# A two-layer graph network on one core: sums of the router weights by one product, and the order of the queues around both routings

## The chip, the core and the metric

The kernel runs on one core of a Trainium2 chip. A core has a matrix engine (PE in the profile, with its weight loads as PEld), a vector engine (DVE), a scalar engine (ACT), a general engine (POOL, GpSimd) and a queue engine (SP) that issues transfers; DVE, ACT, POOL and SP each run their instructions in the order in which they are queued. Sixteen DMA engines move data between the chip's main memory and the core's. The metric is the device time of one execution in microseconds, the median of several runs; less is better.

## The reference

384 nodes with 1024 features pass through two layers, all in float32. Each layer adds two branches to x and then a mixture of experts. Cut to what matters here:

```
xn = layernorm(x)
x = x + graph_attention(xn, edges) + linear_attention(xn)          # layer 0
xn = layernorm(x)
q, k, v = split(xn @ wqkv.T)                                        # 8 columns each
logits = sum(softmax(q[e] * k[j]) * v[j])                           # per expert e
two best experts by logits, weights = softmax of the two logits
x = x + sum(weights * (silu(a) * g) @ w2[e].T),  a, g = xn @ w1[e].T
xn = layernorm(x)                                                   # layer 1
x = x + graph_convolution(xn, W, a, edges) + attention_with_norm(xn)
f = layernorm(x)
e = argmax(f @ centroids.T), alpha = sigmoid of that product
x = x + f + alpha * (relu(xhat * gamma[e] + beta[e]) @ w1[e] ...) @ w2[e] + b2[e] ...
```

Each router works on a normalized row. (x - mean) * rinv @ w is rinv * (x @ w) - mean * rinv * (sum of w over the features), so the kernel multiplies the raw rows with the router's weights and needs the feature sums of the weights once: `wsum` for `wqkv` (24 columns), `csum` for the centroids (8 columns).

## The kernel before

The nodes are three blocks of 128 rows (`nb`), the features eight chunks of 128 (`kc`). Weights stream in 2 MB loads on SP (`load_w`, `load_t`) through a ring of buffers: three to begin with, a fourth (`w_top`), two more (`w_more`) after layer 0's attention, and three more (`w_last`) before layer 1's second routing. A load is issued when the buffer that it takes has been read for the last time. The program is traced in the order of the code; a planner then orders each engine's queue by its own estimates of when operands are ready, so an instruction may stand ahead of others that were traced before it. `tc.issue_after(i)` puts the instructions of its block, on i's engine only, behind i. `held(loads, until)` makes loads wait until another instruction, here a gather, has landed. A pool of tiles opened where another was closed waits for that whole pool by default; with `reuse_waits="tile"` each tile waits only for the tiles that lay where it lies.

The stages that matter, by their times in the profiled execution:

- Start (0 to 17 us). Three blocks of x are loaded and normalized (`norm_on_both`: DVE one half, L204, ACT the other, L205), transposed on PE (`to_t`, L218, copies L219: DVE the first four chunks, ACT the rest) and then multiplied by the first weight (L135). Ahead of the transposes PE multiplies `wr` with a matrix of ones, eight products of 24 columns (L442), and DVE copies the sum to `wsum` (L450).
- First routing (500 to 568 us). For each block, `to_router` (transposes, product with `wr`, norm), `to_places` (`route_block`: the logits from L356 on, an Exp on ACT in L363, both one-hot rows, `both` in L769; `place_both`: the rank of each node from products with triangular and full ones, L387, and the slots, L389 to L400; then POOL scatters the rows to `xg0`) and `to_first` (expert 0's rows gathered by a product, L775). For the last block nothing else is left for PE: it multiplies the centroids with ones, eight products (L789), whose copy to `csum` is L798 on DVE, ranks the nodes, and counts each expert's nodes in `too_many` with a product per block (L344; a maximum on DVE, L346). Then DVE and ACT copy expert 0's rows to `xe0` (L792, L793).
- Experts of layer 0 (`experts0_sorted`, 568 to 699 us). Expert by expert: rows (`rows_of`, POOL loads `xs`, L905), hidden values (L919), then output rows (L972), which go to memory. POOL gathers them back by slot (`take`, L309, summed on DVE in L999); `ways_back` (L937 to L952) prepares tables for the last two experts, which come back by a product (L1041).
- Head of layer 1 (699 to 760 us). Per block: the rows taken back (`take_back`), the norm, transposes (L218), and products with the two halves of `w_gnn` (L1058). The halves were loaded at 673.65 and 678.81.
- Second routing (935 to 976 us). `to_router`, `to_places` and `to_first` of their own (L1197, L1219 to L1230, L1234); `add_normed` on ACT (L193), the gate as a Sigmoid on ACT (L1254), scattered with the node numbers to `ig` by POOL, and `too_many` again.
- Experts of layer 1 (976 us to the end). Pairs of experts; 4 MB of first weights and 4 MB of second weights for each pair. Each product with the first weights (L1371) and the second (L1402) frees buffers for the next loads; the output rows are added to `out` by scatters.

Of the kernel before, what the change touches and what calls it, by code (L numbers as in the profile page):

```python
# [45 lines left out]
def gps_two_layers(ctx: ExitStack, tc: tile.TileContext, d, out: bass.AP):  # L46
# [153 lines left out]
    def norm_on_both(dst, src, mean, rinv):  # L200

        off = small.tile([P, 1], F32, tag="off", name="off")
        ve.tensor_scalar(off, mean, rinv, -1.0, op0=OP.mult, op1=OP.mult)
        first = ve.tensor_scalar(dst[:, :HB], src[:, :HB], mean, rinv, op0=OP.subtract, op1=OP.mult)  # L204
        ac.activation(dst[:, HB:D], src[:, HB:D], AF.Identity, bias=off, scale=rinv)  # L205
        return off, first

# [133 lines left out]
    def too_many(pool, tag, oh, cap):  # L341
        ps = pool.tile([P, HB], F32, tag=tag, name="total")
        for b in range(NB):
            mm(ps[:, :X], lhsT=ones_q, rhs=oh[:, b, :], start=b == 0, stop=b == NB - 1)  # L344
        most = small.tile([P, 1], F32, tag="pl_m", name="pl_m")
        ve.tensor_reduce(most, ps[:, :X], AX.X, OP.max)  # L346
        over = small.tile([P, 1], I32, tag="pl_o", name="pl_o")
        ve.tensor_scalar(over, most, float(cap), None, op0=OP.is_gt)
        return over

    def route_block(ps, sums, off, rinv, apart):
# [6 lines left out]
        qk = small.tile([P, X, X], F32, tag="r_qk", name="r_qk", bufs=1)  # L358
# [3 lines left out]
        ve.tensor_tensor(qk, qk, top[:, :, None].to_broadcast([P, X, X]), OP.subtract)  # L362
        ac.activation(qk, qk, AF.Exp)  # L363
        ready(AF.Sqrt, qk[:, 0, 0:1])
        tot = small.tile([P, X], F32, tag="r_s", name="r_s")
        ve.tensor_reduce(tot, qk, AX.X, OP.add)
        ve.reciprocal(tot, tot)
        ve.tensor_tensor(qk, qk, qkv[:, 2, None, :].to_broadcast([P, X, X]), OP.mult)
        logit = small.tile([P, X], F32, tag="r_l", name="r_l")
        ve.tensor_reduce(logit, qk, AX.X, OP.add)  # L370
# [45 lines left out]
    with ExitStack() as layer:  # L416
# [6 lines left out]
        with tc.tile_pool(name="edges", bufs=1) as ed, tc.tile_pool(name="hot", bufs=2) as hot, \  # L423
# [16 lines left out]
            ps = pa.tile([P, HB], F32, tag="mm", name="sums")  # L440
            for kc in range(KC):
                mm(ps[:, :3 * X], lhsT=ones_q, rhs=wr[:, kc, :], start=kc == 0, stop=kc == KC - 1)  # L442
            ready(AF.Sqrt, eps)
# [5 lines left out]
            with tc.issue_after(copied[0].ins):  # L449
                ve.tensor_copy(wsum, ps[:, :3 * X])  # L450

# [291 lines left out]
        with tc.tile_pool(name="ps_m0", bufs=4, space=PSUM) as pm, \  # L743
# [11 lines left out]
            def to_router(nb):  # L755
                gp.dma_start(x1[nb * P:(nb + 1) * P, :], x[:, nb, :])
                to_t(pm, xT, x[:, nb, :], nb)
                ps = px.tile([P, HB], F32, tag="x", name="x")
                for kc in range(KC):
                    mm(ps[:, :3 * X], lhsT=xT[:, kc, nb * P:(nb + 1) * P], rhs=wr[:, kc, :],  # L760
                       start=kc == 0, stop=kc == KC - 1)
                mean, rinv = norm_block(x[:, nb, :])
                off, _ = norm_on_both(xn[:, nb, :], x[:, nb, :], mean, rinv)
                ready(AF.Exp, xn[:, nb, D - 1:D])
                queries[nb] = (ps, wsum, off, rinv)

            def to_places(nb):
                oh = route_block(*queries[nb], share[:, 1, nb:nb + 1])
                ve.tensor_tensor(both[:, nb, :], oh[0], oh[1], OP.add)  # L769
                place_both(px, slots[:, nb, :], own0[:, nb, :], both, oh, nb)  # L770
                scatter(xg0[:, :], [slots[:, nb, i:i + 1] for i in range(2)], [xn[:, nb, :]] * 2, X * CAP0)

            def to_first(nb):
                for kc in range(KC):
                    mm(first[kc // 4][:, kc % 4, :], lhsT=xn[:, nb, kc * P:(kc + 1) * P], rhs=own0[:, nb, :],  # L775
                       start=nb == 0 and kc % 4 == 0, stop=nb == NB - 1 and kc % 4 == 3)

# [9 lines left out]
            ps = px.tile([P, HB], F32, tag="x", name="sums")  # L787
            for kc in range(KC):
                mm(ps[:, :X], lhsT=ones_q, rhs=cen[:, kc, :], start=kc == 0, stop=kc == KC - 1)  # L789
            to_places(NB - 1)  # L790
            to_first(NB - 1)
            ve.tensor_copy(keep["xe0"][0], first[0])  # L792
            ac.copy(keep["xe0"][1], first[1])  # L793
# [3 lines left out]
            ve.tensor_tensor(share[:, 1, :], share[:, 1, :], share[:, 0, :], OP.mult)  # L797
            ve.tensor_copy(csum, ps[:, :X])  # L798
            over0 = too_many(px, "x", both, CAP0)


# [89 lines left out]
    def experts0_sorted(keep):  # L891

        slots, share = keep["slots"], keep["share"]
        with tc.tile_pool(name="act6", bufs=1) as act, \
                tc.tile_pool(name="work6", bufs=2) as work, \
                tc.tile_pool(name="ps_h6", bufs=5, space=PSUM) as ph, \
                tc.tile_pool(name="ps_t6", bufs=3, space=PSUM) as pt:

# [67 lines left out]
            for hf in range(2):  # L966
# [15 lines left out]
                if hf == 0:  # L982
                    for nb in range(NB):
                        yt = work.tile([P, 2, HB], F32, tag="yt", name="yt6", bufs=3)
                        take(hf, nb, yt, slots, share, X * CAP0)
            take_back(work.tile([P, D], F32, tag="xs", name="yt1").rearrange("p (a b) -> p a b", b=HB), 0)

# [33 lines left out]
    def layer1(keep=None):  # L1021


        with tc.tile_pool(name="act2", bufs=1) as act, \
# [18 lines left out]
            for nb in range(NB):  # L1043
                with ExitStack() as behind:
                    if nb:
                        behind.enter_context(tc.issue_after(normed_half.ins))
                    if keep is not None:
                        if nb:
                            taken = take_back(work.tile([P, 2, HB], F32, tag="xn", name="yt1"), nb)
                        xs = x[:, nb, HB:]  # L1050
                        ve.tensor_tensor(xs, xs, backs[nb], OP.add)
                    mean, rinv = norm_block(x[:, nb, :])
                    _, normed_half = norm_on_both(xn1[:, nb, :], x[:, nb, :], mean, rinv)
                to_t(pm, xnT, xn1[:, nb, :], nb)
                for hf in range(2):
                    ps = pm.tile([P, HB], F32, tag="mm", name="mm")
                    for kc in range(KC):
                        mm(ps, lhsT=xnT[:, kc, nb * P:(nb + 1) * P], rhs=ws[hf][:, kc, :],  # L1058
                           start=kc == 0, stop=kc == KC - 1)
                    ac.copy(hn[:, nb, hf * HB:(hf + 1) * HB], ps)  # L1060
# [126 lines left out]
            own = keep["own"]  # L1187
            sums, last = {}, []

            def to_router(nb):  # L1190
# [350 lines left out]
```

## Time and profile before

| what | value |
|---|---|
| median of 3 runs | 1060.62 us (1059.91 to 1061.09) |
| profiled execution: time | 1058.17 us |
| profiled execution: span on the core | 1056.4 us |
| PE busy | 1019.2 us (96%) |
| DVE, ACT, POOL busy | 356.2, 270.6, 320.3 us |
| mean granted PE clock | 0.986 |
| moved by DMA | 182.83 MB, mean 173 GB/s |
| PE waits, first routing (550 to 590 us) | 2.5, 0.7, 0.5 and 0.4 us |
| PE waits, head of layer 1 (698 to 745 us) | 3.0, 1.9 (three times) and 0.7 us |
| PE waits, second routing and after (940 to 1057 us) | 2.4, 1.9 (twice), 1.4, 1.1 (twice), 0.4 and 0.3 us |

Lines such as L387 are lines of the kernel before. A row of the timeline gives the start, the length, the engine, the line and the operation, what is written and read, and in brackets the idle time before it and what ended that. Equal neighbours are drawn together (x16 is 16 records); one float32 product leaves two records on PE. A row of the table by stretches gives the busy times of PE, PEld, DVE, ACT and POOL with their counts, then the granted PE clock, the mean share of the DMA engines in use, and GB/s. A wait view gives the total, the count and the longest.

### The profile page before, as it was taken

The numbers are of one execution on the slowest core, as the hardware profiler recorded it, in microseconds if no ns is written. First come the engines' busy times: TensorE is split into PE (matmuls) and PEld (weight loads), VectorE is DVE, ScalarE is ACT, GpSimd is POOL, SyncE is SP. The second block draws the span as 40 slices with busy tenths as digits, with TensorE's granted clock in tenths as the row PEclk, the third lists the DMA queues.
The fourth block names the chain that finished last, engine by engine and source line by source line (L and its number), as shares of the span: only waits on it lengthen the run. The fifth ranks groups of instructions, "written<-read, shape, count | busy, mean of one in ns | idle before, by whom it ended". The sixth has DMA issues, their size and how long they took to land. (4 is left out here: it accounts for less than half of the span.)

```text
span 1056.4 us, 9529 instructions
## 1 busy us (share of the span) xinstructions
PE 1019.2 (96%) x3455; PEld 554.2 (52%) x3455; DVE 356.2 (34%) x993; ACT 270.6 (26%) x501; POOL 320.3 (30%) x277
## 2 busy tenths in 40 slices
PE   6999999999999999999998999989999999999995
PEld 5555555554455555544456666434444465656341
DVE  4580000007666766721333111043304100365321
ACT  3111111100776666621112101221212110113210
POOL 2142456566686678510001000050001100001231
PEclk9999999999999999999998999999999999998998
DMA  9939522424424342523155887969622222625994
GB/s 352 398 134 367 156 80 89 151 96 109 80 0 91 71 80 0 160 80 130 61 199 215 306 309 281 373 219 370 228 80 79 80 80 79 241 92 206 309 373 117
DMA packets 69525, 182.83 MB, mean 173 GB/s; under 512 B 21488, under 2 KB 22352, under 8 KB 69216
## 3 DMA queue, kind: packets, MB, share of 16 engines
q1 hardware_dynamic: 41072, 147.58, 38.6%
q0 software_dynamic: 25408, 29.93, 12.3%
q10 hardware_dynamic: 2992, 4.65, 1.2%
q8 instruction: 29, 0.48, 0.2%
q14 instruction: 24, 0.20, 0.1%
HBM read 160.22 MB, written 22.44 MB: 173 GB/s over the span
## 5 line engine op out<-in xcount | busy, mean ns | idle before, releaser
L482 POOL DMA_INDIRECT countd<-seen,cells x96 | 153.4, 1598 | 62.9 <-DMA countd<-seen,cells 37.7
L135 PE MATMUL mm<-xnT,w 128*128 128x384 f32 x512 | 165.7, 486 | 0.1
L135 PEld LDWEIGHTS mm<-xnT,w 128*128 128x128 f32 x512 | 97.1, 190 | 67.7 <-DVE xnT L219 0.4
L668 PE MATMUL mm<-xnT,w 128*128 128x384 f32 x384 | 132.4, 493 | 0.0
L482 POOL DMA_INDIRECT lastd<-typ,cells x96 | 96.7, 1007 | 108.4 <-DMA lastd<-typ,cells 70.9
L668 PEld LDWEIGHTS mm<-xnT,w 128*128 128x128 f32 x384 | 70.5, 190 | 56.4 <-issue 13.4
L716 PE MATMUL mm<-w,t 128*128 128x512 f32 x192 | 84.3, 595 | 0.8 <-DVE x L404 0.8
L147 PE MATMUL mm<-w,xnT 128*128 128x512 f32 x192 | 82.8, 592 | 0.0
L135 PE MATMUL mm<-t,w 128*128 128x384 f32 x256 | 82.7, 486 | 0.0
L919 PE MATMUL h<-w,xeT 128*128 128x352 f32 x224 | 68.5, 462 | 0.7 <-DVE xeT L911 0.4
L135 PEld LDWEIGHTS mm<-t,w 128*128 128x128 f32 x256 | 48.6, 190 | 33.9
L147 PEld LDWEIGHTS mm<-w,xnT 128*128 128x128 f32 x192 | 36.3, 190 | 45.5 <-issue 45.5
L716 PEld LDWEIGHTS mm<-w,t 128*128 128x128 f32 x192 | 35.9, 190 | 44.1 <-issue 42.2
L588 DVE TENSOR_TENSOR kind<-last 128x1152 f32<-128x1152 f32 x1 | 1.4, 1359 | 165.6 <-DMA last<-lastd 165.6
L919 PEld LDWEIGHTS h<-w,xeT 128*128 128x128 f32 x224 | 41.8, 190 | 23.8 <-DVE xeT L911 2.2
L294 POOL DMA_INDIRECT xg<-xn,slot x3 | 4.0, 1330 | 144.6 <-DVE xn L1175 137.6
L1058 PE MATMUL mm<-w,xnT 128*128 128x512 f32 x96 | 43.9, 617 | 1.9 <-DVE xnT L219 1.9
L1164 PE MATMUL mm<-w,oT 128*128 128x512 f32 x96 | 42.6, 595 | 0.0
L972 PE MATMUL y<-w,hT 128*128 128x512 f32 (+1 forms) x96 | 41.6, 592 | 0.0
L147 PE MATMUL mm<-w,t 128*128 128x512 f32 x96 | 41.4, 592 | 0.0
L529 ACT ACTIVATE t<-mm,cols 128x384 f32<-128x384 f32 x24 | 14.0, 581 | 107.0 <-PE mm L135 107.0
L1114 POOL TENSOR_TENSOR x<-x,beta 128x1024 f32<-128x1024 f32 x3 | 7.3, 2428 | 97.5 <-DVE x L1113 97.5
(319 smaller groups left out, 1208.2 us busy)
## 6 DMA issues: line engine op xcount, KB each, us to landing
w<-in_w1s SPq DMA_DIRECT2D x16, 1408.0 KB, 6.8
w<-in_xw2s SPq DMA_DIRECT2D x8, 2048.0 KB, 16.3
w<-in_xw SPq DMA_DIRECT2D x8, 2048.0 KB, 10.6
w<-in_w2s SPq DMA_DIRECT2D x8, 1536.0 KB, 7.3
keys<-keyd POOLq DMA_DIRECT2D x4, 1536.0 KB, 13.7
xg<-blank SPq DMA_DIRECT2D x12, 512.0 KB, 11.3
xs<-xg POOLq DMA_DIRECT2D x10, 512.0 KB, 7.0
w<-in_wk SPq DMA_DIRECT2D x2, 2048.0 KB, 16.0
```

The source lines that it names most:

```text
L135: mm(ps[:, :N], lhsT=w[:, j, kc, :], rhs=rhs[:, kc, :], start=kc == 0, stop=kc == KC - 1)
L147: mm(ps, lhsT=lhs[:, kc, nb * P:(nb + 1) * P], rhs=w[:, kc, :], start=i == 0 and kc == 0, stop=i == len(pairs) - 1 and kc == KC - 1)
L294: i = gp.indirect_dma_start(rows, bass.IndirectOffsetOnAxis(ap=at, axis=0), src, None, bounds_check=n - 1, oob_is_err=False, compute_op=op)
L482: gp.indirect_dma_start(cells[:, :], bass.IndirectOffsetOnAxis(ap=at[:, i, c:c + 1], axis=0), src[:, c:c + 1], None, bounds_check=N * N + ...
L529: ac.activation(dst[:, ob, :], ps, AF.Identity, bias=cols[:, i, ob:ob + 1], scale=1.0)
L668: mm(ps[:, :N], lhsT=w[:, j, kc, :], rhs=xnT[:, kc, :], start=kc == 0, stop=kc == KC - 1)
L716: mm(pss[hf], lhsT=src[:, kc, nb * P:(nb + 1) * P], rhs=w_out[("mwo", "wo")[part]][hf][:, kc, :], start=part == 0 and kc == 0, stop=part = ...
L919: mm(ag[i][:, :F0], lhsT=xeT[kc // 4][:, kc % 4, :], rhs=w1[kc // 4][:, kc % 4, i * F0:(i + 1) * F0], start=kc == 0, stop=kc == KC - 1)
L972: mm(y, lhsT=hT[:k, e, j, :], rhs=w2[:k, e % 2 * len(K2) + j, :], start=j == 0, stop=j == len(K2) - 1)
L1058: mm(ps, lhsT=xnT[:, kc, nb * P:(nb + 1) * P], rhs=ws[hf][:, kc, :], start=kc == 0, stop=kc == KC - 1)
L1114: gp.tensor_tensor(x[:, b, :], x[:, b, :], beta, OP.add)
L1164: mm(ps, lhsT=oT[:, kc, nb * P:(nb + 1) * P], rhs=ws[hf][:, kc, :], start=kc == 0, stop=kc == KC - 1)
```

## The change

- `wsum` and `csum`: one product with ones over all columns (192 and 64), and a reduction over the eight chunks on DVE in place of a copy.
- `too_many`: one product over the three blocks' columns (24), and a reduction over the blocks on DVE before the maximum. In the first routing it is queued behind the last product of `to_first` on PE and behind the copy of `xe0` on DVE, as is the reduction to `csum`.
- `route_block` takes its two tables from the layer's pool, writes the weighted table to a tile of its own, and leaves out the early Sqrt (which loads ACT's table) for the last block.
- The pools of `experts0_sorted` wait by tile.
- Head of layer 1: the second half of `w_gnn` is held until the first block's last gather has landed; a block's DVE work is queued behind the copy of the block before's transposes (`turned[0]`), where it was behind that block's norm.
- Second routing: `add_normed`, and at the end the Sigmoid, are queued behind ACT's half of the norm.

```diff
     def too_many(pool, tag, oh, cap):
         ps = pool.tile([P, HB], F32, tag=tag, name="total")
-        for b in range(NB):
-            mm(ps[:, :X], lhsT=ones_q, rhs=oh[:, b, :], start=b == 0, stop=b == NB - 1)
+        mm(ps[:, :NB * X], lhsT=ones_q, rhs=oh.rearrange("p b e -> p (b e)"), start=True, stop=True)
+        each = small.tile([P, X], F32, tag="pl_e", name="pl_e")
+        ve.tensor_reduce(each, ps[:, :NB * X].rearrange("p (b e) -> p e b", b=NB), AX.X, OP.add)
         most = small.tile([P, 1], F32, tag="pl_m", name="pl_m")
-        ve.tensor_reduce(most, ps[:, :X], AX.X, OP.max)
+        ve.tensor_reduce(most, each, AX.X, OP.max)
...
         ac.activation(qk, qk, AF.Exp)
-        ready(AF.Sqrt, qk[:, 0, 0:1])
+        if more:
+            ready(AF.Sqrt, qk[:, 0, 0:1])
...
-            for kc in range(KC):
-                mm(ps[:, :3 * X], lhsT=ones_q, rhs=wr[:, kc, :], start=kc == 0, stop=kc == KC - 1)
+            mm(ps[:, :KC * 3 * X], lhsT=ones_q, rhs=wr.rearrange("p k c -> p (k c)"), start=True, stop=True)
...
-                ve.tensor_copy(wsum, ps[:, :3 * X])
+                ve.tensor_reduce(wsum, ps[:, :KC * 3 * X].rearrange("p (k c) -> p c k", k=KC), AX.X, OP.add)
...
-            for kc in range(KC):
-                mm(ps[:, :X], lhsT=ones_q, rhs=cen[:, kc, :], start=kc == 0, stop=kc == KC - 1)
+            mm(ps[:, :KC * X], lhsT=ones_q, rhs=cen.rearrange("p k c -> p (k c)"), start=True, stop=True)
             to_places(NB - 1)
-            to_first(NB - 1)
-            ve.tensor_copy(keep["xe0"][0], first[0])
+            summed = to_first(NB - 1)
+            given = ve.tensor_copy(keep["xe0"][0], first[0])
...
-            ve.tensor_copy(csum, ps[:, :X])
-            over0 = too_many(px, "x", both, CAP0)
+            with tc.issue_after(given.ins):
+                ve.tensor_reduce(csum, ps[:, :KC * X].rearrange("p (k c) -> p c k", k=KC), AX.X, OP.add)
+                with tc.issue_after(summed.ins):
+                    over0 = too_many(px, "x", both, CAP0)
...
-        with tc.tile_pool(name="act6", bufs=1) as act, \
+        with tc.tile_pool(name="act6", bufs=1, reuse_waits="tile") as act, \
...
-            take_back(work.tile([P, D], F32, tag="xs", name="yt1").rearrange("p (a b) -> p a b", b=HB), 0)
+            keep["taken"] = take_back(work.tile([P, D], F32, tag="xs", name="yt1").rearrange("p (a b) -> p a b", b=HB), 0)
...
             ws = [load_w(d["w_gnn"][hf]) for hf in range(2)]
+            if keep is not None:
+                held(loads[-1:], keep["taken"])
...
                     if nb:
-                        behind.enter_context(tc.issue_after(normed_half.ins))
+                        behind.enter_context(tc.issue_after(turned[0].ins))
...
-                to_t(pm, xnT, xn1[:, nb, :], nb)
+                turned = to_t(pm, xnT, xn1[:, nb, :], nb)
...
-                norm_on_both(xb, xs, mean, again)
-                add_normed(xs, mean, rinv)
+                normed_by[:] = norm_on_both(xb, xs, mean, again)[1:]
+                with tc.issue_after(normed_by[1].ins):
+                    add_normed(xs, mean, rinv)
...
-            ac.activation(info[:, :, 0], most, AF.Sigmoid)
+            with tc.issue_after(normed_by[1].ins):
+                ac.activation(info[:, :, 0], most, AF.Sigmoid)
```

More of the change, by code (lines that the diff above doesn't have):

```diff
@@ L204, in norm_on_both @@
         first = ve.tensor_scalar(dst[:, :HB], src[:, :HB], mean, rinv, op0=OP.subtract, op1=OP.mult)
-        ac.activation(dst[:, HB:D], src[:, HB:D], AF.Identity, bias=off, scale=rinv)
-        return off, first
+        second = ac.activation(dst[:, HB:D], src[:, HB:D], AF.Identity, bias=off, scale=rinv)
+        return off, first, second
     def normed(dst, src, mv, rinv, nb):
@@ L349, in too_many, with route_block @@
         return over
-    def route_block(ps, sums, off, rinv, apart):
+    def route_block(act, ps, sums, off, rinv, apart, more):
         qkv = small.tile([P, 3, X], F32, tag="r_q", name="r_q")
@@ L357, in route_block @@
         ve.scalar_tensor_tensor(flat, ps[:, :3 * X], rinv, flat, op0=OP.mult, op1=OP.add)
-        qk = small.tile([P, X, X], F32, tag="r_qk", name="r_qk", bufs=1)
+        qk = act.tile([P, X, X], F32, tag="r_qk", name="r_qk")
         ve.tensor_tensor(qk, qkv[:, 0, :, None].to_broadcast([P, X, X]), qkv[:, 1, None, :].to_broadcast([P, X, X]), OP.mult)
@@ L367, in route_block @@
         ve.reciprocal(tot, tot)
-        ve.tensor_tensor(qk, qk, qkv[:, 2, None, :].to_broadcast([P, X, X]), OP.mult)
+        given = act.tile([P, X, X], F32, tag="r_g", name="r_g")
+        ve.tensor_tensor(given, qk, qkv[:, 2, None, :].to_broadcast([P, X, X]), OP.mult)
         logit = small.tile([P, X], F32, tag="r_l", name="r_l")
-        ve.tensor_reduce(logit, qk, AX.X, OP.add)
+        ve.tensor_reduce(logit, given, AX.X, OP.add)
         ve.tensor_tensor(logit, logit, tot, OP.mult)
@@ L762, in to_router @@
                 mean, rinv = norm_block(x[:, nb, :])
-                off, _ = norm_on_both(xn[:, nb, :], x[:, nb, :], mean, rinv)
+                off = norm_on_both(xn[:, nb, :], x[:, nb, :], mean, rinv)[0]
                 ready(AF.Exp, xn[:, nb, D - 1:D])
@@ L767, in to_places @@
             def to_places(nb):
-                oh = route_block(*queries[nb], share[:, 1, nb:nb + 1])
+                oh = route_block(act, *queries[nb], share[:, 1, nb:nb + 1], nb < NB - 1)
                 ve.tensor_tensor(both[:, nb, :], oh[0], oh[1], OP.add)
@@ L774, in to_first @@
                 for kc in range(KC):
-                    mm(first[kc // 4][:, kc % 4, :], lhsT=xn[:, nb, kc * P:(kc + 1) * P], rhs=own0[:, nb, :],
-                       start=nb == 0 and kc % 4 == 0, stop=nb == NB - 1 and kc % 4 == 3)
+                    i = mm(first[kc // 4][:, kc % 4, :], lhsT=xn[:, nb, kc * P:(kc + 1) * P], rhs=own0[:, nb, :],
+                           start=nb == 0 and kc % 4 == 0, stop=nb == NB - 1 and kc % 4 == 3)
+                return i
             for nb in range(1, NB):
@@ L893, in experts0_sorted @@
         slots, share = keep["slots"], keep["share"]
-        with tc.tile_pool(name="act6", bufs=1) as act, \
-                tc.tile_pool(name="work6", bufs=2) as work, \
-                tc.tile_pool(name="ps_h6", bufs=5, space=PSUM) as ph, \
-                tc.tile_pool(name="ps_t6", bufs=3, space=PSUM) as pt:
+        with tc.tile_pool(name="act6", bufs=1, reuse_waits="tile") as act, \
+                tc.tile_pool(name="work6", bufs=2, reuse_waits="tile") as work, \
+                tc.tile_pool(name="ps_h6", bufs=5, space=PSUM, reuse_waits="tile") as ph, \
+                tc.tile_pool(name="ps_t6", bufs=3, space=PSUM, reuse_waits="tile") as pt:
             hT = act.tile([P, X, len(K2), CAP0], F32, name="hT6")
@@ L1052, in layer1 @@
                     mean, rinv = norm_block(x[:, nb, :])
-                    _, normed_half = norm_on_both(xn1[:, nb, :], x[:, nb, :], mean, rinv)
-                to_t(pm, xnT, xn1[:, nb, :], nb)
+                    norm_on_both(xn1[:, nb, :], x[:, nb, :], mean, rinv)
+                turned = to_t(pm, xnT, xn1[:, nb, :], nb)
                 for hf in range(2):
@@ L1187, in layer1 @@
             own = keep["own"]
-            sums, last = {}, []
+            sums, last, normed_by = {}, [], []
             def to_router(nb):
```

## The prediction

> **What bounds the kernel now.** I read the page first, then the waits of PE, then the timeline of the places where PE waits, then the clock in stretches of 1 us, then landing times by tile.
>
> ```profile
> PE 1019.2 (96%) x3455; PEld 554.2 (52%) x3455; DVE 356.2 (34%) x993; ACT 270.6 (26%) x501; POOL 320.3 (30%) x277
> ...
> PE rank L387 <- DVE both L769: 2.5, 1, 2.5
> PE y L1402 <- SPq L1439: 2.4, 1, 2.4
> ```
>
> PE is busy in 96% of the span, so only three kinds of thing can pay: work taken from PE, a wait of PE, and time at half clock. The page's clock row dips at four places: the tail of the first routing, the head of layer 1, the tail of the second routing, the end. In two of them PE's wait is one that the change touches.
>
> First the tail of the first routing (timeline of DVE, then ACT, then PE; start, length, instruction, idle before it):
>
> ```profile
> 555.31 0.23 DVE L362 TENSOR_TENSOR r_qk<-r_qk,r_t 128x64 f32<-128x64 f32 x1
> 558.64 0.17 DVE L798 COPY csum<-sums 128x8 f32<-128x8 f32 x1 [3.11 <-PE sums L789]
> 558.73 0.21 DVE L366 TENSOR_REDUCE r_s<-r_qk 128x8 f32<-128x64 f32 x1
> ...
> 561.79 0.17 DVE L769 TENSOR_TENSOR both<-r_o 128x8 f32<-128x8 f32 x1
> ...
> 556.16 0.24 ACT L363 ACTIVATE r_qk<-r_qk 128x64 f32<-128x64 f32 x1
> ...
> 562.01 0.60 PE L387 MATMUL rank<-both,later 128*128 128x8 f32 x2 [2.51 <-DVE both L769]
> ...
> 563.55 3.78 PE L775 MATMUL first<-own,xn 128*128 128x128 f32 x16 [0.51 <-DVE own L390]
> 568.01 11.79 PE L919 MATMUL h<-w,xe 128*128 128x352 f32 x32 [0.68 <-ACT xe L793]
> ```
>
> See the queue of DVE: L366 needs only the Exp of ACT, done at 556.40, yet starts at 558.73, because the copy of csum stands ahead of it and waits for the eight products of L789. Everything down to `both` is late by that, and PE with it. And the clock:
>
> ```profile
> 561.00:562.00 1.00, 0.00 (x0) 0.00 (x0) 0.85 (x6) 0.21 (x1) 0.00 (x0) 0.97 0.00 0
> ...
> 571.00:572.00 1.00, 1.00 (x3) 0.64 (x2) 0.60 (x4) 0.00 (x0) 0.28 (x1) 0.50 0.00 0
> ```
>
> The seventh number is the granted clock: half from 561.9 to about 572.1.
>
> Then the head of layer 1:
>
> ```profile
> 709.52 0.75 DVE L999 SCALAR_TENSOR_TENSOR x<-yt,share_g,x 128x512 f32<-128x512 f32 x1 [1.04 <-DMA yt<-yg,slots_g]
> ...
> 710.79 0.67 DVE L219 COPY xnT<-mm 128x512 f32<-128x512 f32 x1
> ...
> 708.53 1.84 PE L218 MATMUL mm<-ident,xn 128*128 128x128 f32 x8 [3.04 <-DVE xn L204]
> 711.52 15.98 PE L1058 MATMUL mm<-w,xnT 128*128 128x512 f32 x32 [1.15 <-DVE xnT L219]
> ```
>
> The same fault: the copy that PE waits for stands behind the next block's first sum, which waits for its gather. After 984 the kernel is bound by its loads (DMA share near 1.0 to 1037, PE waits for the last weights). That stage is started by PE: the load at 984.21 takes the buffer that the first experts' h (to 984.18) gives up, and from 976 to 979 the DMA share was 0.02 to 0.03. So time won on PE before 984 moves the whole end.
>
> **Part by part.** The sum is against the profiled execution (1058.17 us, span 1056.4, so 1.8 outside it), which lies 2.45 below the median of the runs, 1060.62; I carry the difference over to the median.
>
> *Feature sums at the start.* 16 records of L442 (8 products; from 7.73 to 11.31) become 2 of 192 columns. No row has that shape; records here stand 0.22 apart at 24 columns and 0.33 at 384 (10.27 for 31 of L135), twice that at half clock: 0.4 to 1.3 us in all, I take 0.7. Either ends well before the first normed block is there (DVE L204, 9.63 + 0.54), so the price doesn't matter: L218 starts at 10.2 instead of 11.13, 0.9 earlier, and the third block's norm follows, since DVE had it behind the copies of the transposes. DVE's wsum becomes a reduction of 192 elements (0.17 before; 0.22 for 64 elements, 0.69 for a copy of 512; I take 0.35), ahead of the edge tables, which PE does not meet for 250 us. Here a rule speaks against the change. The row: L218 took 3.65 us for 16 records at 11.13, and 1.04 for 8 at 503.38, so PE was still slow after 3.4 us of L442. The Trainium skill, "TensorE: Matmul & The Clock Gate", "Part 1: The HAM clock gate", says that about 3.4 us of sustained activity release the clock; by it, taking 2.9 us of activity away moves full speed back by up to one window, 3.4 us at half speed, 1.7 lost, and this part would be a loss of 0.8. By the row the small products did not warm PE, and the gain is 0.9. I take 0.8, nearest to the row; ends -0.8 and 0.9.
>
> *First routing, tail.* (a) csum goes behind the copy of xe0: L366 starts at 556.45, 2.3 earlier, `both` is there at 559.7. PE's own work shrinks too (the 16 records of L789, 556.76 to 558.61, to about 0.3 us), but it then only waits longer. (b) L346 no longer stands between L389 (562.65) and L390 (563.16): 0.3, so L775 begins at about 561.0 instead of 563.55: 2.6 with (a). (c) The pools of the sorted experts wait by tile: h reads xe0's first half, which DVE copies (0.69) while PE works on the second; its PSUM banks are long free. The wait of 0.68 goes. (d) The count is now one product behind L775, ahead of h or within it; its PSUM buffer needs csum reduced first. Before, it lay in waits. Bounds 0.1 (the product beside h) and 0.5 (0.25 product, 0.25 wait for the reduction behind L792); I take 0.4. The two extra reductions on DVE (0.16 to 0.22 each) lie beside h. (e) The missing Sqrt preload and the separate tile `given` free ACT of two table loads of 1.28 in a stretch where it idles: nothing; if that cover were gone, 1.28. (f) The clock. The stretch without dense products was 556.8 to 563.55, 6.8 us; it becomes 556.8 to 561.0, 4.2. At half clock L775 took 3.78 against some 2.05 (16 at 1.04 / 8), and h 11.79 against 9.8 (68.5 us for 224 of the same shape): 3.7 lost. The skill's rule (same section) is that an idle window of 3.4 us halves the clock and that the windows run free; by it 4.2 still holds a whole window in about a quarter of the phases, and 3.7 would mostly come back. The rows are harsher: PE stood idle 3.04 before 708.53 and the clock fell at 708.7. So I give 4 in 10 to no halving (3.7 back) and else 0.5 (full speed comes back sooner, PE being fed without a gap): 1.9 taken, ends 0.5 and 3.7. Sum 2.6 + 0.7 - 0.4 + 1.9 = 4.8; ends 3.3 and 6.9.
> What is late next: the rows of expert 1. POOL's two scatters (565.24 and 567.01, landing 4.0 after the second) and the load xs (571.72, 4.1 to landing) follow the slots by 11.3 us (564.46 to 575.8). The slots come at 561.9, so xs is there at 573.2; at full clock h ends at 573.0. It just fits.
>
> *Head of layer 1.* (a) The second block's DVE work goes behind `turned[0]`: the copy starts when four transposes are done, 709.5, and L1058 when PE is through with them, 710.4 instead of 711.52: 1.1. Queued behind the copy is the whole second block (two sums, norm, to 715 before, some 716 now); its transposes come at 727, so 10 us hide it. The third block starts behind the second copy (728) and takes 5 us before it is due at 742.6; L1070 moves back by as much, with the k projection ahead of its reader. (b) `held`: the second half of w_gnn leaves SP at about 704.9 (gather landed at 700.81 + 3.5) instead of 678.8. SP has nothing behind it but w_k, already held to 713.8. Alone, 2048 KB land in 7.9 (w_q); beside 1 MB of gathers, 10: 715. It is due at product 9 of L1058: 710.4 + 8 x 0.88 to 1.75, past 717.5. Covered by 2.5; uncovered, each us is a us. What it brings: gathers took 4.6 to 6.2 beside it and 3.4 to 3.5 without, but the ones on PE's path (699.51, 700.81) already ran without it (it landed at 692.6). Left is the last row store, 0.2; ends 0 and 0.6. (c) Clock: half from 708.7 to 715.5; a shorter gap gives 0.2, ends 0 and 1.7. Sum 1.5; ends 0.3 (half of (a) lost to the order of the queue, a little to the weight) and 3.4.
>
> *Second routing.* The Sigmoid (0.21, and its table load 1.28) goes behind the last L205, which starts 0.4 sooner; PE needs that half only four products after `slot` (972.17), and POOL's scatter waits for `slot` as well: nothing. The info scatters on POOL (from 974.19) then wait for info until about 974.6: 0.4 later, and with them xs, inf and the three b2 gathers; xs (landed 983.0) is read at 985.4, loads fill the DMA engines meanwhile. The count's third DVE step sits in the chain before L1227: 0 to 0.15. Taken 0; ends -0.6 and 0.4.
>
> Sum: 0.8 + 4.8 + 1.5 + 0 = 7.1 us. Profiled execution 1051.1, median 1060.62 - 7.1 = 1053.5. All ends together: 2.2 to 11.6.
>
> **Rivals.** *A: the order gives it back.* With waits by tile, the tables L937 to L950 on DVE (571.29 to 574.77, 3.5 us) can start once the slots are there and stand ahead of the copy of xe0, and the clock is halved as before. For it: on DVE L598 was run at 10.78, far ahead of its use, so early work is put in gaps. Against: the steps are short and fill gaps. Then 7.1 - 1.4 - 2.5 = 3.2 gained: 1057.4.
> *B: nothing arrives.* The end is bound by loads (182.83 MB in all), and an earlier PE would only wait longer for them. Against: DMA was idle at 976 to 979 and the first of the last loads waits for PE. Then 1060.6, give or take 1.
> *C: slower, the held weight.* L1058 needs w_gnn's second half at 718. If it shares the engines with gathers, a_bc, ed_w, gamma, beta and w_k and lands 22 us after its issue, at 727, PE waits 9 us and the clock falls again (2 more): 7.1 - 11 gives 1064.5. It decides from a landing at about 723, where the loss equals the gain. For: w_k's loads took 17.9 (median). Against: those were queued behind one another; this one starts on idle engines (DMA share 0.00 at 705 to 707).
>
> **How the numbers follow.** Forecast 0.64 (1049 to 1057), A 0.20 (1055.5 to 1059), B 0.08, C 0.08. Below 0.2%, 2.1 us, this kernel can hardly be told from no change. Faster: forecast and A, 0.84; same 0.08; slower 0.08. The range takes in the ends of the costs and A: 1048.8 to 1059.
>
> **What would show it.** L366 within 0.2 of ACT's L363; PE's wait for `both` still near 2, but L775 ready 2.5 sooner; h right behind L775; half clock for 7 us or less there; L1058 behind L218 without a wait; w_gnn's second landing before 717; L218 at the start at 10.2. I am wrong if csum or the tables still stand ahead of L366 or L792, if PE waits for w_gnn, or if the time from the first h of layer 1's experts to the end grows.

## The result, and the profile after

The changed kernel takes 1049.83 us in the median (1046.98 to 1052.54, 6 runs), the kernel before 1060.56 (1058.29 to 1061.28, 6 runs) beside it. The ratio is 0.9904, 95% interval 0.9884 to 0.9923: faster by 1%, 10.7 us between the medians. The profiled executions are closer: 1058.17 before, 1050.11 after, 8.06 us apart. The table of stages below is made for that pair.

The page of the changed kernel, part 1, and its waits of PE (total, count, longest):

```profile
PE 1011.5 (96%) x3419; PEld 547.2 (52%) x3419; DVE 355.5 (34%) x995; ACT 267.7 (26%) x498; POOL 320.7 (31%) x277
```

```profile
PE mm L218 <- DVE xn L204: 3.9, 2, 3.4
PE h L1379 <- SPq L1447: 2.3, 1, 2.3
PE rank L390 <- DVE both L771: 2.0, 1, 2.0
```

PE is busy 7.7 us less, nearly all of the 8.2 us that the span lost (1056.4 to 1048.3). The wait for `both` has only fallen from 2.5 to 2.0. What moved is the time at which it ends.

At the start the transposes (L218) and the first weight's products (L135) begin earlier; one row before, two after (a length is that of the records up to 20 us):

```profile
16.96 3.49 PE L135 MATMUL mm<-xnT,w 128*128 128x384 f32 x10
...
10.31 3.59 PE L218 MATMUL mm<-ident,xn 128*128 128x128 f32 x16 [1.55 <-DVE off L203]
...
15.90 4.46 PE L135 MATMUL mm<-xnT,w 128*128 128x384 f32 x13
```

The timeline of the first routing's tail (DVE, then PE):

```profile
555.37 0.22 DVE L368 TENSOR_REDUCE r_s<-r_qk 128x8 f32<-128x64 f32 x1 [0.90 <-ACT r_qk L364]
555.51 0.22 DVE L371 TENSOR_TENSOR r_g<-r_qk,r_q 128x64 f32<-128x64 f32 x1
...
558.25 0.17 DVE L771 TENSOR_TENSOR both<-r_o 128x8 f32<-128x8 f32 x1
...
561.33 0.69 DVE L794 COPY xe<-first 128x512 f32<-128x512 f32 x1 [0.91 <-PE first L777]
561.94 0.21 DVE L801 TENSOR_REDUCE csum<-sums 128x8 f32<-128x64 f32 x1
...
559.50 3.50 PE L777 MATMUL first<-own,xn 128*128 128x128 f32 x16 [0.64 <-DVE own L393]
562.79 0.46 PE L343 MATMUL total<-both,ones_q 128*128 128x24 f32 x2
563.08 9.79 PE L923 MATMUL h<-w,xe 128*128 128x352 f32 x32
572.71 1.04 PE L914 MATMUL t<-ident,xs 128*128 128x128 f32 x8
```

The sum of the exponentials (L368, L366 before) now waits for ACT and no longer for `csum`, which is reduced behind the copy of expert 0's rows. `both` is there 3.54 us earlier, 1.06 of them from the start. h begins 4.93 us earlier and right behind the count, and it takes 9.79 us where it took 11.79. In the table by stretches, whose seventh number is the granted clock:

```profile
559.00:560.00 1.00, 0.50 (x3) 0.50 (x4) 0.86 (x6) 0.00 (x0) 0.00 (x0) 0.92 0.04 16
562.00:563.00 1.00, 1.00 (x7) 1.00 (x6) 0.15 (x2) 0.00 (x0) 0.18 (x2) 0.50 0.31 127
563.00:564.00 1.00, 1.00 (x5) 0.79 (x5) 0.60 (x5) 0.95 (x2) 0.93 (x1) 0.87 0.97 397
```

Half clock lasts from 559.8 to 563.2, one stretch of 3.4 us where there were 10.2, and h has full speed from its first products on. The head of layer 1 (PE, then DVE):

```profile
701.86 1.10 PE L218 MATMUL mm<-ident,xn 128*128 128x128 f32 x8 [3.35 <-DVE xn L204]
703.31 15.63 PE L1064 MATMUL mm<-w,xnT 128*128 128x512 f32 x32 [0.35 <-DVE xnT L219]
...
702.56 0.69 DVE L219 COPY xnT<-mm 128x512 f32<-128x512 f32 x1 [0.75 <-PE mm L218]
...
706.29 0.75 DVE L1003 SCALAR_TENSOR_TENSOR x<-yt,share_g,x 128x512 f32<-128x512 f32 x1 [3.04 <-DMA yt<-yg,slots_g]
```

The copy is ahead of the next block's sum, and the product waits 0.35 us for it instead of 1.15. 

The table shows where the profiled pair gained. Each stage is read on PE, from one mark to the next, in both profiles: the first product with the first weight, the begin of the last eight products of `to_first`, the end of h, the end of layer 0's experts, the transposes of the head's second block, the end of the first h of layer 1, the end of the span. The clock's part is what those eight products and h take less in length.

| stage | forecast, us | measured, us |
|---|---|---|
| start, up to the first weight | 0.8 | 1.06 |
| first routing: order of DVE's queue | 2.6 | 2.99 |
| first routing: waits by tile, less the count | 0.3 | 0.60 |
| first routing: clock | 1.9 | 2.28 |
| head of layer 1 | 1.5 | 1.59 |
| second routing | 0 | 0.18 |
| last 73 us | 0 | -0.59 |

The rest of layer 0's experts gave 0.06. Together 8.16 us, the difference of the spans. The 0.18 of the second routing is not one of order: its last eight products begin 11.24 us behind the stage before, 11.23 before the change, and the h behind them takes 8.12 us instead of 8.30.

### The profile page after: what moved, and what is told of

Read it like the earlier page. It is cut to its first block, busy times and chain, and to the rows that moved or that the text cites. A ratio compares the mean times of both kernels' runs of the same rounds, so it can differ in the third digit from the quotient of the medians.

```text
span 1048.3 us, 9455 instructions
## 1 busy us (share of the span) xinstructions
PE 1011.5 (96%) x3419; PEld 547.2 (52%) x3419; DVE 355.5 (34%) x995; ACT 267.7 (26%) x498; POOL 320.7 (31%) x277
## 5 line engine op out<-in xcount | busy, mean ns | idle before, releaser
L135 PE MATMUL mm<-xnT,w 128*128 128x384 f32 x512 | 165.7, 486 | 0.0
L135 PEld LDWEIGHTS mm<-xnT,w 128*128 128x128 f32 x512 | 97.2, 190 | 67.4 <-DVE xnT L219 0.2
L135 PE MATMUL mm<-t,w 128*128 128x384 f32 x256 | 82.7, 486 | 0.0
L135 PEld LDWEIGHTS mm<-t,w 128*128 128x128 f32 x256 | 48.7, 190 | 33.9
```

The costliest lines, as they stand in the source:

```text
L135: mm(ps[:, :N], lhsT=w[:, j, kc, :], rhs=rhs[:, kc, :], start=kc == 0, stop=kc == KC - 1)
```

## Experiments

Ratios are to the kernel before, run beside each. Line numbers are those of the kernel shown.

**The kernel before, profiled again.** No edit.

> The kernel before, profiled once more. Its median lay 2.4 us above its profiled execution (1060.56 against 1058.17). Theory: the half-clock stretches fall differently in each execution (free-running windows), so another profile shows the same queue and waits (PE waiting 2.5 for both, 0.7 for xe0, 3.0 and 1.2 at the head of layer 1) but other half-clock stretches, 10.2 + 6.8 + 6.8 us before 1000 us now, up to 3.4 us more or less in each place; time 1058 to 1062. Rival: the extra lies in the loads at the end, and the time from the first h of layer 1's experts to the end (73.3 us in the profile, 975.9 to 1049.2) is longer by 2.

It took 1059.76 us, with a span of 1058.0. From the end of the first h of layer 1 to the end of the span it needed 72.46 us, against 72.27 in the first profile and 72.86 in the changed kernel: in this pair a start 9 us earlier (975.4 against 984.2) lengthens the last stage by 0.6. Over all profiles here the stage took 72.1 to 76.4 us, and 74.57 in the second profile of the changed kernel. This profile also shows that the same kernel loses differently from run to run. Half clock ended sooner, h took 9.73 us, and then PE waited for expert 1's rows:

```profile
567.84 9.73 PE L919 MATMUL h<-w,xe 128*128 128x352 f32 x32 [0.68 <-ACT xe L793]
580.38 1.94 PE L910 MATMUL t<-ident,xs 128*128 128x128 f32 x8 [2.80 <-issue]
```

**`csum` and the count's maximum behind the copy on DVE, alone.** The eight products stay.

```diff
-            ve.tensor_copy(keep["xe0"][0], first[0])
+            given = ve.tensor_copy(keep["xe0"][0], first[0])
...
-            ve.tensor_copy(csum, ps[:, :X])
-            over0 = too_many(px, "x", both, CAP0)
+            with tc.issue_after(given.ins):
+                ve.tensor_copy(csum, ps[:, :X])
+                over0 = too_many(px, "x", both, CAP0)
```

> Kernel before with one edit: csum's copy and the maximum of the count stand behind the copy of xe0 on DVE; the eight and three products stay. Theory (the order of DVE's queue makes the gain at the first routing): L366 starts right behind ACT's Exp (556.5 instead of 558.7), both is there 2.2 us sooner; PE's own small products (L789 to 558.6, L387 to 559.0) still end before it, so L775 starts 2.5 sooner; with what the clock gives 2.5 to 5 us faster. Rival (fewer products make it): PE is busy with them until 559 and the gain is under 1 us.

1057.28 us, ratio 0.9978 (0.9965 to 0.9992). The last eight products of `to_first` begin at 562.72, 0.8 us earlier than before (0.1 of it from an earlier start), and not the 2.5 that the order should bring. The timeline (DVE, then PE) says why:

```profile
556.19 0.22 DVE L366 TENSOR_REDUCE r_s<-r_qk 128x8 f32<-128x64 f32 x1 [0.90 <-ACT r_qk L363]
...
557.80 0.23 DVE L368 TENSOR_TENSOR r_qk<-r_qk,r_q 128x64 f32<-128x64 f32 x1 [1.15 <-ACT none L198]
...
561.42 1.45 PE L344 MATMUL total<-both,ones_q 128*128 128x8 f32 x6 [0.26 <-DVE pb_r L389]
```

L366 is early, as forecast. But L368 writes over the table of exponentials that ACT's early Sqrt (L198) still has to read, and that operation stands behind a table load: 1.15 us. And the count's three products are now ahead of the gathering products on PE, 1.45 us. In the change, the separate table and the missing Sqrt take away the first and the place behind `to_first` the second.

**The sums by one product each, alone.** Nothing is requeued.

```diff
-            for kc in range(KC):
-                mm(ps[:, :X], lhsT=ones_q, rhs=cen[:, kc, :], start=kc == 0, stop=kc == KC - 1)
+            mm(ps[:, :KC * X], lhsT=ones_q, rhs=cen.rearrange("p k c -> p (k c)"), start=True, stop=True)
```

with the reductions, and the same for `wsum` and the count.

> Kernel before with the three sums by one product each, nothing requeued. csum's reduction stays ahead of L366 on DVE, but now waits for one product behind L775's first two blocks. Theory: the start gains 1.0 (as in the kernel after), the wait of DVE ends at about 557.1 less the 1.0 instead of 558.6, so the routing gains 1.5 of the 2.3, less 0.1 for a third counting step on DVE ahead of the own row: 2.5 us, and up to 3 more by the clock: 2.5 to 5. Rival (only the order counts): 1 us at the start and nothing at the routing.

1056.38 us, ratio 0.9968 (0.9955 to 0.998): about a third of the gain. The last eight products begin at 562.04, 1.5 us earlier than before. Of this 0.4 is the start; the other 1.1 come because `csum` is ready sooner (reduced at 556.70, copied at 558.64 before). h ends 3.7 us earlier, and half clock there lasted 6.8 us instead of 10.2. So the shorter sum of the centroids is more than work taken from a wait: where `csum` stays ahead of L366, it shortens the chain itself.

**The changed kernel with eight products for `wsum`.**

```diff
-            mm(ps[:, :KC * 3 * X], lhsT=ones_q, rhs=wr.rearrange("p k c -> p (k c)"), start=True, stop=True)
+            for kc in range(KC):
+                mm(ps[:, :3 * X], lhsT=ones_q, rhs=wr[:, kc, :], start=kc == 0, stop=kc == KC - 1)
```

> Kernel after with the eight products for wsum at the start. Theory: L218 starts at 11.1 instead of 10.3 and L135 at about 17.0 instead of 15.9; 1.0 us slower than the kernel after, the rest unchanged: 9 to 10 us faster than before. Rival (the eight products warm PE up sooner): L218 and the first of L135 run faster and the time is that of the kernel after or better.

1051.45 us, ratio 0.9936 (0.9917 to 0.9955), intervals that still touch. The first weight's products begin at 17.32 against 15.90: the start is worth 1.42 here, 1.06 in the profiled pair. All profiles agree on the direction: in the four with eight products those of the first weight begin at 16.84 to 17.32, in the ten with one product at 15.85 to 16.52. Beyond that, half clock at the first routing lasted 6.8 us in this profile instead of 3.4.

**The changed kernel with pools that wait as a whole.**

```diff
-        with tc.tile_pool(name="act6", bufs=1, reuse_waits="tile") as act, \
+        with tc.tile_pool(name="act6", bufs=1) as act, \
```

and so for the other three.

> Kernel after with the pools of the sorted experts waiting for the whole closed pool again. Theory: h waits for ACT's copy of xe0's second half and for the count's steps on DVE: L777 to h is 0.7 to 1.2 us longer, and the clock may stay at half a window (3.4 us) longer; 0.7 to 2.5 us slower than the kernel after. Rival (h needs both halves anyway): no change.

1051.13 us, ratio 0.9911 (0.9896 to 0.9926), not to be told from the change. In the profile h starts 0.68 us behind the last gathering product (562.75 against 562.07), and 0.08 in the changed kernel: the term exists, and its 0.6 us are below what the times resolve. Half clock lasted 6.8 us there instead of 3.4.

**The changed kernel with the head's old order.** A block's DVE work goes behind the norm of the block before; the weight stays held.

```diff
-                        behind.enter_context(tc.issue_after(turned[0].ins))
+                        behind.enter_context(tc.issue_after(normed_half.ins))
```

> Kernel after with the second block's DVE work behind the first block's norm again. Theory: the first sum of block 2 stands ahead of the copy of xnT, and its gather lands later than in the kernel before, because the held weight is now in flight beside it (in the kernel after that sum waited until 706.3, while the copy ran at 702.6): the copy moves to 706.3 + 1.4 and PE waits some 4 us more there; 3 to 6 us slower than the kernel after. Rival (the copy's place costs what it cost before): 1.1 us slower.

1057.62 us, ratio 0.9981 (0.9968 to 0.9993): most of the gain is gone, 7.8 us by the medians, more than the 3 to 6 expected. Of the 7.7 us between the spans of the two profiles the head makes 4.3; the start makes 0.5, a longer half clock at the first routing 1.1 and the last stage 1.9, which this edit does not touch. From the end of layer 0's experts to the first product with `w_gnn` pass 15.3 us, against 10.9 in the changed kernel and 12.1 before.

```profile
707.34 0.75 DVE L1003 SCALAR_TENSOR_TENSOR x<-yt,share_g,x 128x512 f32<-128x512 f32 x1 [4.41 <-DMA yt<-yg,slots_g]
...
708.61 0.68 DVE L219 COPY xnT<-mm 128x512 f32<-128x512 f32 x1
...
709.34 11.17 PE L1064 MATMUL mm<-w,xnT 128*128 128x512 f32 x22 [5.26 <-DVE xnT L219]
```

The copy stands behind a sum that waits 4.41 us for the second block's gather, and PE waits 5.26 us. The held load leaves at 698.88, into that gather: it is summed 13.3 us after the experts' end, against 10.1 before the change. So with the hold the old order is 3.2 us worse than before the change (1.6 to 3.3 us worse than in the four profiles with the old order and no hold, where 12.0 to 13.7 us pass), and the new order is what makes the hold harmless.

**The changed kernel without the hold.**

```diff
-            if keep is not None:
-                held(loads[-1:], keep["taken"])
```

> Kernel after without the hold on the second half of w_gnn. Theory: the two gathers on PE's path run without the load either way; no change within 0.5 us, the gathers of blocks 2 and 3 land sooner (3.5 us instead of up to 7) with nobody waiting. Rival (the hold is what speeds the head of layer 1): 1 to 2 us slower.

1052.04 us, ratio 0.9918 (0.9904 to 0.9932), again inside the scatter. From the experts' end to the first product pass 11.2 us, against 10.9. That difference of 0.3 us is no measure of the hold: six profiles with the hold and the new order show 10.1 to 11.7.

**The changed kernel with the second routing as before.**

```diff
-                with tc.issue_after(normed_by[1].ins):
-                    add_normed(xs, mean, rinv)
+                add_normed(xs, mean, rinv)
```

and the Sigmoid likewise.

> Kernel after with add_normed and the Sigmoid of the second routing not queued behind the norm. Theory: PE's wait for slot (1.4) and the start of h there do not move; no change within 0.5 us; the Sigmoid's table load stands ahead of ACT's half of the last norm again. Rival (the norm's second half feeds PE's last products and POOL's scatter): 0.5 to 1 us slower.

1050.89 us, ratio 0.9913 (0.99 to 0.9927). The last eight products begin 11.22 us after the last product of the stage before, against 11.24 in the changed kernel. Nothing, as forecast.

**The changed kernel with filler products.** Ten products of 128x384 that nobody reads keep PE at work in the three tails: three behind the sum of the centroids, four behind the last product of the way back, three around the second routing's last rank.

```diff
+            fill(pm, 3, summed)
...
+                fill(pm, 4, gone)
...
+                if nb == NB - 1:
+                    fill(pm, 1, i)
...
+            fill(pm, 2, ranked[0])
```

> Kernel after with ten products of 128x384 that nobody reads, in places where PE waits: three behind csum's product, four behind the products of the way back at the head of layer 1, one and two around the rank of the second routing. The results are those of the reference. Theory (half clock follows from PE's idle stretches): the clock stays at full in all three places; L777 takes 2.1 instead of 3.5, the first eight products at the head of layer 1 run at full speed (1.7 saved), the second routing's L1241 2.1 instead of 3.8 and the first h there 7.1 instead of 8.1: 4 to 6 us faster than the kernel after, less up to 0.5 where a product stands in the way. Rival (half clock follows from something else, or the fillers delay what PE waits for): same or slower than the kernel after.

1052.0 us, ratio 0.9929 (0.991 to 0.9947): not faster than the change, against the 4 to 6 us expected. In the profile full clock was kept in all three places (`to_first` took 2.05 us instead of 3.50) and h ended at 571.30 instead of 572.87. Then PE stood still. The timeline of PE, SP and POOL:

```profile
574.04 1.94 PE L924 MATMUL t<-ident,xs 128*128 128x128 f32 x8 [2.74 <-DMA xs<-xg]
...
566.60 17.19 SPq L124 DMA_DIRECT2D w<-in_w1s  x3
...
567.03 1.15 POOL L919 DMA_DIRECT2D xs<-xg  x2 [3.05 <-PE h L933]
```

and in the changed kernel:

```profile
568.17 16.39 SPq L124 DMA_DIRECT2D w<-in_w1s  x4
...
566.98 1.15 POOL L909 DMA_DIRECT2D xs<-xg  x2 [3.06 <-issue]
```

The rows leave at the same time, 567.0. But h at full speed from its start gives its first weight buffer back sooner, and the next weight (1408 KB) leaves at 566.60, ahead of the rows, instead of 568.17, behind them. The rows then land at about 574.0, 7.0 us after their issue; in the changed kernel they are there by 572.7. Behind PE's 2.74 us of waiting the clock is half for 6.8 us in the middle of dense products:

```profile
574.00:575.00 1.00, 0.96 (x5) 0.99 (x6) 0.00 (x0) 0.00 (x0) 0.00 (x0) 0.50 1.00 385
```

From h's end to the end of layer 0's experts it took 125.1 us, against 119.5: the 1.6 us gained cost 5.6. The profile of the kernel before taken again has the same order: weight at 572.88, rows at 573.71, a wait of 2.80 us, though there the rows left 2 us later as well. In its first profile the rows left first (571.72, weight 575.09), and PE did not wait.

**The changed kernel again,** beside the fillers.

> The kernel after once more, beside the one with fillers on the same chip. Theory: 10 to 11 us faster than before, with half-clock stretches at the same three places but of one or two windows of 3.4 us each as it falls. Rival: the first measurement was a lucky draw and the gain is that of the profiled pair, 8.

1049.08 us, ratio 0.9907 (0.9889 to 0.9925): the first result is confirmed. By the medians it is 9.6 us, between the 10 to 11 of the theory and the 8 of the rival.

**Fillers at the head of layer 1 and at the second routing only.** The edit is shown against the kernel with all ten.

```diff
-            fill(pm, 3, summed)
```

> The kernel after with unread filler products only at the head of layer 1 (four behind the last product of the way back) and around the second routing's last rank (one before it, two behind it); none at the first routing. With fillers in all three places the head and the second routing kept full clock, but PE reached the end of the first h at 571.3 and then waited 2.7 us for the rows of expert 1. Theory (the clock there is real time, and only the rows of expert 1 ate the gain): the first h ends at about 572.9 as in after, no wait over 1 us for the rows, no half clock from 575 to 1000; the first product of layer 1 runs some 44.6 us over its three blocks where it took 46.2, the second routing's last eight products take about 2.1 where they took 3.8; 2 to 4 us faster than after: 1045.5 to 1048, ratio 0.986 to 0.989. Rival (whatever is won is taken back by the loads of the last experts, which pace the last 70 us): the times up to 975 move by 3 us, the time does not: 1049 to 1051, ratio about 0.991.

1046.95 us (1046.02 to 1047.34), ratio 0.9893 (0.9878 to 0.9907), the lowest median of all. Weight and rows leave as in the changed kernel (568.02 and 566.81), and PE does not wait for the rows. At the head:

```profile
698.20 2.74 PE L332 MATMUL fill<-rowf,ident 128*128 128x384 f32 x8
700.77 1.04 PE L218 MATMUL mm<-ident,xn 128*128 128x128 f32 x8
702.16 14.00 PE L1075 MATMUL mm<-w,xnT 128*128 128x512 f32 x32 [0.35 <-DVE xnT L219]
```

The fillers lie in the wait and end before the transposes are due; the first block's products take 14.00 us instead of 15.63, and the three blocks are done 2.6 us sooner after the experts' end (1.0 from an earlier begin, 1.6 from 44.6 us instead of 46.2). That is no proof for the fillers: without any, the profile of the run with the second routing as before has 14.00 us too, and its three blocks are done as soon. The other profiles without fillers and with the changed order have 14.7 to 16.2 us. At the second routing half clock did not vanish, against the theory: it fell to one stretch of 3.4 us from 6.8, which the changed kernel taken again shows without fillers, and there the first h of layer 1 ended 0.5 us sooner behind the stage before. The last stage, 72.2 us, took no longer than before, so the rival is not supported. By the medians this is 2.1 to 2.9 us better than the changed kernel, by the ratios to the kernel run beside each 1.2 to 1.5; the ratios' intervals overlap, so only the direction is likely, not the size, and by which of the fillers is open.

**The changed kernel with one table and the early Sqrt put back.**

```diff
-        if more:
-            ready(AF.Sqrt, qk[:, 0, 0:1])
+        ready(AF.Sqrt, qk[:, 0, 0:1])
...
-        given = act.tile([P, X, X], F32, tag="r_g", name="r_g")
+        given = qk
```

> The kernel after, with the last block's early Sqrt put back and the weighted table written over the table of exponentials, as before the change; all else of the change stays. The prediction priced this part at nothing, since ACT idles there. The run that only put csum behind the copy of expert 0's rows contradicts it: DVE waited 1.15 us for the small ACT operation that reads the table. Theory (csum's place is worth its 2.3 us only together with this part): DVE's product with the values waits 1.1 to 1.2 us for ACT, both and the rank come 1.2 to 1.5 us later than in after (559.4 to 559.8 instead of 558.25), the stretch without dense products grows from 3.8 to about 5.2 us and half clock may take a second window; 1.2 to 3 us slower than after: 1050.5 to 1053, ratio 0.992 to 0.994. Rival (as the prediction had it, nothing): both within 0.2 of 558.25, the ratio that of after, 0.9904.

1053.16 us (1047.63 to 1056.56), ratio 0.9935 (0.9916 to 0.9954), 3.3 us above the changed kernel's first median; the ratios' intervals overlap. DVE's row, and PE's:

```profile
557.56 0.23 DVE L370 TENSOR_TENSOR r_qk<-r_qk,r_q 128x64 f32<-128x64 f32 x1 [1.15 <-ACT none L198]
...
561.76 3.78 PE L776 MATMUL first<-own,xn 128*128 128x128 f32 x16 [0.64 <-DVE own L392]
```

The wait of 1.15 us is back, `both` comes at 560.31 instead of 558.25 (0.6 of that from a later start of the stage), and half clock takes 6.8 us again. Counted from the first weight's products, h ends 2.1 us later than in the changed kernel, and 0.8 to 1.0 later than in the profiles of the changed tail that also drew 6.8 us of half clock. The rival, nothing, has fallen.

## Why the prediction was right, and where not

**The direction and the mechanism held.** DVE's queue order was the cause in both places, at the first routing only together with the part named below. L368 begins 0.03 us after ACT's Exp ends (555.34), PE still waits 2.0 for `both`, h follows the count without a wait, transposes at the start begin at 10.31 (forecast 10.2). The tables of `ways_back` start at 563.78, behind the copy and the reductions: rival A did not come. PE never waits for `w_gnn`, so rival C did not either. The last stage lengthened by 0.6 in the pair and 2.3 in the changed kernel's second profile, not by all that PE gained, so rival B fell; but a growth of this stage was one of the prediction's signs of being wrong, and in this small size it came.

**The step that failed is (e) of the first routing.** The prediction priced the separate table and the missing Sqrt at nothing, since ACT idles there, and at 1.28 us only if that cover were gone. ACT does idle; but DVE's next product overwrites the table that ACT's Sqrt reads, so DVE waits for it. Before, that wait was covered by the late `csum`; when `csum` leaves, it appears: 1.15 us in two profiles. With the clock, h ends 0.8 to 2.1 us later by it; the 3.3 us in the times are not clear of the noise. The 2.3 us given to (a) belong to (a) and (e) together. The sum stood only because both are in the change.

**Terms that were mis-sized.** The order of the first routing brought 2.99 us for 2.6, the count cost 0.1 instead of 0.4 (0.46 us of records, of which most lies beside the neighbours), the clock gave 2.28 for 1.9: one stretch of half clock was left, neither none nor nearly all. All err in the same direction, and the profiled pair gained 8.1 for 7.1.

The 1.9 was near by luck. The prediction's own weights give 1.8, neither of its two cases came, and the term is a draw. Of the seven profiles with this tail and no fillers at it, four had one stretch of half clock and three had two, which cost another 1.2 us. Against the second profile of the kernel before, which drew 6.8 us instead of 10.2, the clock gave nothing.

The head's 1.5 was right to 0.1, 1.23 of it up to the first product and 0.36 after; this too is closer than the scatter allows, since the first product comes 10.1 to 11.7 us behind the experts in six profiles with the new order, by when the gathers land and how fast PE runs. One reading was wrong: the page's clock row shows three of the four dips, and the head's shows only in the stretches of 1 us.

**The medians moved further, 10.7 us, than the profiled pair.** The prediction carried the offset of the profiled execution (2.45 us under its median) over to the kernel after. It did not carry: after's profile lay at its median. Part of the offset was a draw: in the four later series (11 to 23 runs each) the median of the kernel before was 1058.66 to 1059.49, only 0.5 to 1.3 us above its profile. The profile of the kernel before taken again, 1.6 us slower, contains a loss that the first has not, 2.80 us of waiting for expert 1's rows and a halved clock in dense products, and the changed kernel's two profiles do not have it. How often each kernel meets it was not measured, so this is a possible cause of the rest and not a shown one.

**"It just fits" was right, and thinner than it looked.** PE went on to expert 1's rows without a wait (572.71). With h 1.6 us faster it had to wait for them, because the weight load overtook them (2.74 us, the run with all ten fillers).

**The rule on the start.** By the rule of the Trainium skill ("TensorE: Matmul & The Clock Gate", "Part 1: The HAM clock gate") as the prediction weighed it, the shorter sum at the start should have lost 0.8 us; it gained 1.06, and undoing it alone lost 1.42. As the prediction's row said, the 24-column products had not brought full speed.

## What to carry to other kernels

When a copy leaves the head of an in-order queue, look at once for the next wait that it covered, here a buffer that another engine still reads: 1.15 us that no row of the old profile showed. A faster engine gives buffers back earlier, and the loads that this starts can overtake the one transfer that the engine needs next; compare the issue times of the two before taking more from the engine. Idle time just before dense work can be paid twice, as a wait and as half clock. Unread products in the gap kept full clock at the first routing and at the head; that they pay in time is likely, not shown, and only where what comes next is already there. Where a term hangs on the clock, take several profiles of both kernels before giving it a size: one pair made it 2.28 us, another none.

## What the runs showed of the hardware

- Half clock came in stretches of 3.4, 6.8 or 10.2 us in every profile up to the last 20 us. In each profile all changes of the granted clock lie whole multiples of 3.41 us apart, as if on a grid (in the changed kernel it falls at 559.84, 703.20 and 962.61), and the grid lies elsewhere in each run. A fall of the clock went with PE's idle time between two lines of the grid, by the profile's records. Outside the two routings, in 14 profiles up to 15 us before the end, the clock fell behind each of the 20 such windows with 2.03 us or more of idle time, and behind none with 2.01 or less. So a wait of 2.30 us (1017.4 to 1019.7, changed kernel) was enough, as it lay inside one window, while one of 3.00 us (1024.5 to 1027.5, the run with the head's old order) was not, as a line cut it into 1.84 and 1.16. The whole idle window of about 3.4 us by which the Trainium skill ("TensorE: Matmul & The Clock Gate", "Part 1: The HAM clock gate") has the clock fall was not needed; the measurement decides.
- The same tail drew 3.4 or 6.8 us in different runs. That is not all of the 5.6 us between the runs of the changed kernel: its fastest run has the highest mean clock (0.993 at 1046.98 us), but the two slowest have 0.992 (1052.12 and 1052.54 us) and the three between them 0.989 or 0.990. What the slowest lost is open; they have no profile.
- PE counted as busy does not keep the clock. In the last kernel with fillers PE was idle for only 0.15 us in the window that ends at 959.5. In it lay products of eight columns, one filler and the begin of a second, and the clock still fell. In the second profile of the kernel before it fell at 559.8 behind a window with 0.10 us of idle time, most of it products of eight columns.
- At the start the profile's clock stands at 1.00 while sixteen records of transposes take 3.59 us; eight take 1.04 later. That slowness isn't in the clock row.
